# A seam between two network layers: x1 written over the head values, two row tiles held back, and stores and row sums moved to other queues

## The chip, the cores and the metric

The kernel runs on one core of a Trainium2 chip. TensorE multiplies matrices, VectorE and ScalarE do elementwise work, GpSimd and SyncE are used here for little but issuing transfers. The metric is the device time of one execution in microseconds, as the median of several runs.

## What is computed

Eight batches of 2048 rows of 256 features go through two layers, each followed by an addition of its input and a layer norm. All batches share one 2048 x 2048 adjacency mask.

```python
# layer 0: additive attention, 8 heads of 32 features
e    = leaky_relu(e_src[..., :, None] + e_dst[..., None, :], 0.2) + softplus(beta) * log(adj + 1e-6)
attn = softmax(where(adj > 0, e, lowest))
x1   = layernorm(x + concat_heads(attn @ x_proj) @ W_out.T)
# layer 1: dot-product attention
e2   = leaky_relu((x1 @ W1) @ (x1 @ W2).T, 0.2)
out  = layernorm(x1 + relu(softmax(where(adj > 0, e2, -1e12)) @ (x1 @ W3)))
```

## The kernel before

**Layer 0** (class `Gat`, one object per batch). `project` makes the projected values `v` and the factors `re` and `c`; for batches 1 to 7 this is done ahead, during batch 0, and the results are put aside in device memory (`v_d`, `re_d`, `c_d`). The main loop has 64 units per batch: 4 head pairs (`hp`) times 16 tiles of 128 source rows (`jt`). A unit (`step`) loads a 1 MB tile `mt` of the mask's factors, VectorE makes one tile `s` of 128 x 2048 for each of the two heads (L311, from a pool of four buffers), and TensorE multiplies them by the values into `val` (PSUM) and by the weights of the row sums into `den` (L336). For some `jt` the row sums are gathered instead by VectorE and ScalarE in two tiles `d` (L318, L324), which TensorE adds at the end.

After a head pair's 16th unit comes `finish`: ScalarE copies `val` to `ht` and `den` to `dn`; four small transfers put the row sums into `rc` (L353), VectorE takes the reciprocal (L354), one transfer stores it to `rec_d` (L355), and after every second head pair four transfers spread it over the partitions as `rb` (L361), with which VectorE multiplies `ht` (L363). `rb` and `d` share a pool of two buffers.

`output` has 16 row tiles. For each, TensorE multiplies `ht` by the output weights (`y`, L376), VectorE adds x (L378), which was loaded into the tile `h3` (L372), `layer_norm` runs (two VectorE instructions, five on ScalarE, L202 to L210), and x1 goes to device memory (`x1_d`, L380). `turn` then transposes each row tile of x1 into `x1t` (L391, L392) and multiplies by W3 (L396); the result takes the place of x1 in `h3` (L398). `h3` and `x1t` have one buffer each.

**Layer 1** (class `Dot`). For each of 16 row tiles, `scores` makes `e` on TensorE (L426), ScalarE puts it through the leaky relu into `p` (L428), VectorE adds the mask and takes the maximum (L431), and ScalarE takes the exponential (L432). `step` transposes `p` in four groups (`pt`, L445), which ScalarE copies out of PSUM (`pts`, L447), and multiplies by `h3` into `acc` (L461). Between the first group and the product it makes the scores of the next row tile. An epilogue (L464 to L471) divides, applies relu, adds x1, normalises and stores.

**The order.** TensorE executes in the order in which the program writes its instructions. A scheduler orders the other engines and the queues when the kernel is built, by the same priorities and its estimates. `step` of `Dot` takes a function `fill(k)` that is called at three places in it, and with which units of layer 0 of the next batch are put between the parts of layer 1 of this one. The work at a change of batch, from the last head pair's end to the first step of the new `Dot`, is called the seam here. There one row tile of the old `Dot` is held back, to be done first:

```python
if dot is not None:
    dot.step()
layer_0(2)
for k, _ in enumerate(gat.output()):
    if k % 8 == 7:
        layer_0(1)
for k, _ in enumerate(gat.turn()):
    if k % 2 == 1:
        layer_0(1)
```

In the first seam there is no `Dot` yet, and in the last no further batch, so `layer_0` does nothing there. Every transfer is issued by SyncE, from one queue in order.

Of the kernel before, what the change touches and what calls it, by code (L numbers as in the profile page):

```python
# [9 lines left out]
F32 = mybir.dt.float32  # L10
# [8 lines left out]
P = 128  # L19
# [8 lines left out]
def kernel(  # L28
# [26 lines left out]
    nc = tc.nc  # L55
    B, N, D = x.shape
    H, _, DH = w_proj.shape
    NT = N // P
    KC = D // P
    BK = 512  # L60
    NB = N // BK
    HALF = N // 2
    HP = 2
    NP = H // HP
    IG = BK // P
# [5 lines left out]
    whole = ctx.enter_context(tc.tile_pool(name="whole", bufs=1))  # L71
    wide = ctx.enter_context(tc.tile_pool(name="wide", bufs=2))
    chunk = ctx.enter_context(tc.tile_pool(name="chunk", bufs=2))
# [4 lines left out]
    def mm_tile(name):  # L78
        return ps.tile([P, BK], F32, tag="mm", name=name)

    def wide_tile(name, tag, bufs, dtype=F32):
        return wide.tile([P, N], dtype, tag=tag, name=name, bufs=bufs)
# [6 lines left out]
    ident = const.tile([P, P], F32)  # L89
# [39 lines left out]
    wot = const.tile([P, KC, D], F32)  # L129
# [28 lines left out]
    v_d = dram.tile([B, P, NT, D], F32, name="v_d")  # L158
    re_d = dram.tile([B, P, 2, NT, H], F32, name="re_d")
    rec_d = dram.tile([B, NP, 4, HALF], F32, name="rec_d")  # L160
    x1_d = dram.tile([B, N, D], F32, name="x1_d")
# [37 lines left out]
    def layer_norm(z):  # L199

        st = small.tile([P, nc.vector.BN_STATS_DIM], F32, name="st", bufs=2)
        nc.vector.bn_stats(st, z)  # L202
        mv = small.tile([P, nc.vector.BN_AGGR_DIM], F32, name="mv", bufs=3)
        nc.vector.bn_aggr(mv, st)  # L204
        f = small.tile([P, 4], F32, name="f", bufs=3)
        nc.scalar.activation(f[:, 0:1], mv[:, 1:2], AF.Ln, bias=eps_ln)  # L206
        nc.scalar.activation(f[:, 1:2], f[:, 0:1], AF.Exp, scale=-0.5)
        nc.scalar.mul(f[:, 2:3], mv[:, 0:1], -1.0)
        nc.scalar.activation(f[:, 3:4], f[:, 1:2], AF.Identity, scale=f[:, 2:3])
        nc.scalar.activation(z, z, AF.Identity, bias=f[:, 3:4], scale=f[:, 1:2])  # L210

    def row_tile(name, bufs=4):
        return small.tile([P, D], F32, tag="row", name=name, bufs=bufs)


    class Gat:


        def __init__(self, b):
            self.b = b  # L220
            self.units = ((hp, jt) for hp in range(NP) for jt in range(NT))
            self.hts = []
            self.mts = []

        def project(self):
# [56 lines left out]

        def load(self):
            self.v = whole.tile([P, NT, D], F32, name="v")
            nc.sync.dma_start(self.v, v_d[self.b])
            self.re = small.tile([P, 2, NT, H], F32, name="re", bufs=2)
            nc.sync.dma_start(self.re, re_d[self.b])

        def query_rows(self, h):

# [49 lines left out]
        def finish(self, hp):  # L340


            b, lo = self.b, hp % 2 * HP * DH
            if lo == 0:
                self.hts.append(whole.tile([P, N], F32, name=f"ht{hp // 2}"))
            ht = self.hts[-1]
            for s in range(2):
                nc.scalar.copy(ht[lo:lo + HP * DH, ts(s, HALF)], self.val[ts(s, HP * DH), :])
            dn = chunk.tile([P, HALF], F32, tag="ht", name="dn", bufs=3)
            nc.scalar.copy(dn, self.den)  # L350
            rc = small.tile([P, HALF // DH], F32, name="rc", bufs=1)
            for q in range(4):
                nc.sync.dma_start(rc[ts(q, DH), :], dn[q * DH:q * DH + 1, :])  # L353
            nc.vector.reciprocal(rc, rc)  # L354
            nc.sync.dma_start(rec_d[b, hp].rearrange("q (p c) -> (q p) c", c=HALF // DH), rc)  # L355
            if lo == 0:
                return
            rb = wide_tile("rb", "d", 2)
            for a in range(2 * HP):
                src = rec_d[b, hp - 1 + a // HP, a % HP::HP, :]  # L360
                nc.sync.dma_start(rb[ts(a, DH), :].rearrange("p (s i) -> p s i", s=2),  # L361
                                  bass.AP(tensor=src.tensor, offset=src.offset, ap=[[0, DH]] + list(src.ap)))
            nc.vector.tensor_mul(ht, ht, rb)  # L363

        def output(self):


            b = self.b
            self.h3 = h3 = whole.tile([P, NT, D], F32, tag="h3", name="h3")
            xb = x[b].rearrange("(t p) d -> p t d", p=P)  # L370
            for g in range(NB):
                nc.sync.dma_start(h3[:, ts(g, IG), :], xb[:, ts(g, IG), :])  # L372
            for it in range(NT):
                y = mm_tile("y")
                for g, ht in enumerate(self.hts):
                    nc.tensor.matmul(y[:, 0:D], ht[:, ts(it, P)], wot[:, g, :], start=(g == 0), stop=(g == 1))  # L376
                z = h3[:, it, :]
                nc.vector.tensor_add(z, y[:, 0:D], z)  # L378
                layer_norm(z)
                nc.sync.dma_start(x1_d[b, ts(it, P), :], z)  # L380
                yield

        def turn(self):

            self.x1t = x1t = whole.tile([P, KC, N], F32, tag="x1t", name="x1t")
            h3 = self.h3
            for it in range(NT + 1):
                if it < NT:
                    t = mm_tile("tr1")
                    for kc in range(KC):  # L390
                        nc.tensor.transpose(t[:, ts(kc, P)], h3[:, it, ts(kc, P)], ident)  # L391
                    nc.scalar.copy(x1t[:, :, ts(it, P)], t[:, 0:D].rearrange("p (k i) -> p k i", k=KC))  # L392
                if it > 0:
                    t = mm_tile("h3p")
                    for kc in range(KC):
                        nc.tensor.matmul(t[:, 0:D], x1t[:, kc, ts(it - 1, P)], w3s[:, kc, :],  # L396
                                         start=(kc == 0), stop=(kc == KC - 1))
                    nc.scalar.copy(h3[:, it - 1, :], t[:, 0:D])  # L398
                    yield


    class Dot:
# [32 lines left out]
        def step(self, fill=lambda k: None):  # L435


            it, (p, den) = self.at, self.ahead
            self.at += 1
            fill(0)  # L440

            def turned(g):
                t = mm_tile("pt")
                for k in range(IG):
                    nc.tensor.transpose(t[:, ts(k, P)], p[:, ts(g * IG + k, P)], ident)  # L445
                pt = chunk.tile([P, BK], F32, tag="pt", name="pts", bufs=2)
                nc.scalar.copy(pt, t)  # L447
                return pt

            pt = turned(0)  # L450
            if it + 1 < NT:
                if (it + 1) % IG == 0:
                    self.queries((it + 1) // IG)
                self.scores(it + 1)
            fill(1)
            acc = pacc.tile([P, D], F32, tag="acc", name="acc")
            for g in range(NB):
                now, pt = pt, turned(g + 1) if g + 1 < NB else None
                for k in range(IG):
                    j = g * IG + k  # L460
                    nc.tensor.matmul(acc, now[:, ts(k, P)], self.h3[:, j, :], start=(j == 0), stop=(j == NT - 1))  # L461
            fill(2)
            rec = small.tile([P, 1], F32, name="rec1", bufs=2)
            nc.vector.reciprocal(rec, den)  # L464
            xr = row_tile("x1r")
            nc.sync.dma_start(xr, x1_d[self.b, ts(it, P), :])
            z = row_tile("z")
            nc.scalar.activation(z, acc, AF.Relu, scale=rec)  # L468
            nc.vector.tensor_add(z, z, xr)  # L469
            layer_norm(z)  # L470
            nc.sync.dma_start(out[self.b, ts(it, P), :], z)  # L471


    gats = [Gat(b) for b in range(B)]
# [15 lines left out]
    dot = None  # L490
    for b in range(1, B + 1):
        gat, fresh = gats[b - 1], gats[b] if b < B else None

        def layer_0(count):
            if fresh:
                fresh.step(count)

        if fresh:
            fresh.load()
        if dot is not None:  # L500
            dot.step()
        layer_0(2)
        for k, _ in enumerate(gat.output()):
            if k % 8 == 7:
                layer_0(1)
        for k, _ in enumerate(gat.turn()):
            if k % 2 == 1:
                layer_0(1)
        dot = Dot(gat)
        dot.step(lambda k: layer_0((2, 1, 1)[k]))  # L510
        for i in range(NT - 2):
            dot.step(lambda k: layer_0((0, 2 - (i % 2 == 1), 2 - (i % 14 == 13))[k]))
    dot.step()


# [29 lines left out]
```

## Time and profile before

| | |
|---|---|
| time, median of 3 | 4468.5 us (4466.72 to 4468.73) |
| span of the profiled execution | 4465.4 us |
| TensorE, VectorE, ScalarE, GpSimd busy | 96%, 81%, 39%, 0% |
| granted TensorE clock, mean | 0.984 |
| moved by transfers | 843.62 MB, 189 GB/s |

The times in the views are microseconds, durations in groups of instructions nanoseconds. A line of the waits reads: engine and line that waited, the instruction it waited for, the total, how often, and the longest. A line of the timeline reads: start, duration, engine, line, operation, result <- operands, count of merged instructions, and in brackets the idle time before them. `SPq` is SyncE's queue of transfers, and its duration is that of the issue alone. A line `A:B` of the table of stretches gives the length, and then each engine's busy time in it with the number of instructions.

### The profile page before, as it was taken

Reading aid. Unit: us, or ns where it says so; the run is one execution under the profiler, and the core shown is the slowest. Engines: PE = TensorE matmul, PEld = TensorE weight load, DVE = VectorE, ACT = ScalarE, POOL = GpSimd, SP = SyncE. Lnnn points to the kernel's source line nnn. Section 1 sums busy time; section 2 is a strip of 40 time slices with the busy share of each in tenths; the row PEclk is TensorE's granted clock in tenths of the full one; section 3 lists DMA queues with packets and bytes.
Section 4 is the critical chain, followed back from the end, with each engine's and each line's share of the span. In section 5 each row is a group of like instructions: output and inputs, shape, how many; then the busy total and the mean of one; then the engine's idle time right before and its main releaser. Section 6 shows DMA issues by size and latency. Waiting matters only on the chain.

```text
span 4465.4 us, 60558 instructions
## 1 busy us (share of the span) xinstructions
PE 4267.6 (96%) x24988; PEld 2217.3 (50%) x24988; DVE 3631.8 (81%) x2605; ACT 1758.7 (39%) x3611; POOL 7.5 (0%) x14
## 2 busy tenths in 40 slices
PE   6899899999999999999999999999999999999899
PEld 4444344445455545555455544545454554554566
DVE  5778798888989988988899888888988888898222
ACT  5622233334333343334333343333433343333555
POOL 0000000000000000000000000000000000000000
PEclk8999999999999999999999999999999999999999
DMA  7777665666555555556555565555545565553211
GB/s 217 262 264 263 249 218 204 220 233 217 180 189 193 182 193 184 188 181 224 176 182 178 186 213 187 189 181 207 194 160 190 189 216 183 187 182 134 69 50 41
DMA packets 252773, 843.62 MB, mean 189 GB/s; under 512 B 33616, under 2 KB 152400, under 8 KB 176976
## 3 DMA queue, kind: packets, MB, share of 16 engines
q1 hardware_dynamic: 252496, 839.74, 54.0%
q8 instruction: 196, 3.21, 0.3%
q14 instruction: 81, 0.66, 0.0%
HBM read 763.76 MB, written 75.37 MB: 188 GB/s over the span
## 4 chain that ended last, share of the span: by engine, by line
PE 60%; DVE 14%; issue 8%; ACT 4%; DMA 1%; SPq 0%; DVEq 0%; ACTq 0%
PE acc L461 17%; PE e L426 15%; PE val L336 12%; DVE s L311 9%; PE den L336 8%; PE pt L445 4%; DVE d L318 3%; PE h1p L416 2%; ACT p L432 1%; PE h3p L396 1%; ACT h L210 1%; DVE p L431 1%; PE y L376 1%; DMA mt<-mt_d 0%; ACT f L206 0%
## 5 line engine op out<-in xcount | busy, mean ns | idle before, releaser
L311 DVE SCALAR_TENSOR_TENSOR s<-c,re,mt 128x2048 f32<-128x2048 f32 x1024 | 2350.6, 2343 | 209.6 <-PE den L336 159.9
L336 PE MATMUL val<-s,v 128*32 128x512 f32 x8192 | 1045.3, 607 | 78.7 <-DVE s L311 78.5
L461 PE MATMUL acc<-h,pts 128*128 128x256 f32 x4096 | 950.6, 380 | 14.9 <-ACT pts L447 14.4
L426 PE MATMUL e<-x1t,h 128*128 128x512 f32 x2048 | 904.0, 594 | 0.0
L461 PEld LDWEIGHTS acc<-h,pts 128*128 128x128 f32 x4096 | 748.2, 190 | 107.7 <-ACT pts L447 21.8
L336 PE MATMUL den<-s,re 128*32 128x512 f32 x5568 | 709.2, 598 | 0.0
L318 DVE SCALAR_TENSOR_TENSOR d<-s,re,d 128x2048 f32<-128x2048 f32 x272 | 632.4, 2343 | 0.0
L426 PEld LDWEIGHTS e<-x1t,h 128*128 128x128 f32 x2048 | 379.6, 190 | 450.1 <-issue 417.9
L336 PEld LDWEIGHTS val<-s,v 128*32 128x32 f32 x8192 | 240.9, 110 | 697.8 <-issue 526.3
L447 ACT COPY pts<-pt 128x512 f32<-128x512 f32 x512 | 296.1, 583 | 664.7 <-PE pt L445 664.4
L428 ACT ACTIVATE p<-e 128x512 f32<-128x512 f32 x512 | 302.5, 595 | 432.3 <-PE e L426 432.3
L431 DVE CUSTOM_DVE_ANT_0 p<-p,pen 128x2048 f32<-128x2048 f32 x128 | 292.7, 2287 | 205.9 <-ACT p L428 205.6
L336 PEld LDWEIGHTS den<-s,re 128*32 128x32 f32 x5568 | 194.2, 112 | 426.7 <-issue 426.6
L432 ACT ACTIVATE p<-p,neg 128x2048 f32<-128x2048 f32 x128 | 256.7, 2005 | 272.5 <-DVE neg L431 272.5
L445 PEld LDWEIGHTS pt<-ident,p 128*128 128x128 f32 x2048 | 238.0, 141 | 223.5 <-issue 167.2
L445 PE MATMUL pt<-ident,p 128*128 128x128 f32 x2048 | 318.7, 279 | 5.4 <-ACT p L432 5.4
L469 DVE TENSOR_TENSOR z<-z,x1r 128x256 f32<-128x256 f32 x128 | 54.0, 422 | 205.4 <-ACT z L468 197.0
L468 ACT ACTIVATE z<-acc,rec 128x256 f32<-128x256 f32 x128 | 60.6, 473 | 355.9 <-PE acc L461 330.3
L376 PE MATMUL y<-wot,ht 128*128 128x256 f32 x512 | 129.6, 414 | 37.4 <-DVE ht L363 36.3
L206 ACT ACTIVATE f<-mv,eps_ln 128x1 f32<-128x1 f32 x256 | 74.2, 290 | 199.0 <-DVE mv L204 198.1
L396 PE MATMUL h3p<-w3s,x1t 128*128 128x256 f32 x512 | 133.4, 386 | 12.3 <-ACT x1t L392 12.3
L376 PEld LDWEIGHTS y<-wot,ht 128*128 128x128 f32 x512 | 104.7, 208 | 68.3 <-DVE ht L363 39.2
(76 smaller groups left out, 2083.6 us busy)
## 6 DMA issues: line engine op xcount, KB each, us to landing
mt<-mt_d SPq DMA_DIRECT2D x496, 1024.0 KB, 4.8
c<-c_d SPq DMA_DIRECT2D x64, 1024.0 KB, 6.7
pen<-pen_d SPq DMA_DIRECT2D x112, 512.0 KB, 3.3
xr<-in_x_dram SPq DMA_DIRECT2D x16, 1024.0 KB, 7.1
adj_t<-in_adj_dram SPq DMA_DIRECT2D x16, 1024.0 KB, 6.8
mt_d<-mt SPq DMA_DIRECT2D x16, 1024.0 KB, 5.6
rb<-rec_d SPq DMA_DIRECT2D x64, 256.0 KB, 4.0
h<-in_x_dram SPq DMA_DIRECT2D x32, 512.0 KB, 5.9
```

The lines of the kernel that those rows point to most:

```text
L311: nc.vector.scalar_tensor_tensor(sa, self.cs[a], self.re[:, 0, jt, h:h + 1], mt, ALU.max, ALU.mult)
L318: nc.vector.scalar_tensor_tensor(d, sa, e[:, jt - 1, h:h + 1], d, ALU.mult, ALU.add)
L336: nc.tensor.matmul(dst[ts(q, DH), ts(c, BK)], weights[q % 2], s[q % 2][:, ds(q // 2 * HALF + c * BK, BK)], start=start, stop=stop)
L376: nc.tensor.matmul(y[:, 0:D], ht[:, ts(it, P)], wot[:, g, :], start=(g == 0), stop=(g == 1))
L396: nc.tensor.matmul(t[:, 0:D], x1t[:, kc, ts(it - 1, P)], w3s[:, kc, :], start=(kc == 0), stop=(kc == KC - 1))
L426: nc.tensor.matmul(t, self.h1[:, kc, ts(it % IG, P)], self.x1t[:, kc, ts(c, BK)], start=(kc == 0), stop=(kc == KC - 1))
L428: nc.scalar.activation(p[:, ts(c, BK)], t, AF.Prelu, alpha=ALPHA)
L431: nc.vector.tensor_tensor_reduce(p, p, pen, -1.0, FMAX, ALU.add, ALU.min, neg)
L432: nc.scalar.activation(p, p, AF.Exp, bias=neg, scale=-1.0, accum_out=den)
L445: nc.tensor.transpose(t[:, ts(k, P)], p[:, ts(g * IG + k, P)], ident)
L447: nc.scalar.copy(pt, t)
L461: nc.tensor.matmul(acc, now[:, ts(k, P)], self.h3[:, j, :], start=(j == 0), stop=(j == NT - 1))
```

## The change

Four things are done together.

1. x1 is written over the head values. `ht` of both head groups becomes one tile, laid out so that the 256 columns that row tile `it` read of it are contiguous (`self.ht[:, it]`), and `output` writes x1 into them. x comes through tiles `xg` from the pool `ht` of small tiles (three buffers). `h3` is not needed until `turn`, so `output` doesn't wait for the old `Dot` to be done with it.
2. Two row tiles of layer 1 are held back for the seam. The first (with the last scores in it) is done with two layer-0 units at its end; into the second the 16 row tiles of `output` are put as 5, 5 and 6, with two units. The remaining units are spread over 13 steps rather than 14.
3. ScalarE issues the stores of x1 and of the output, and the four transfers `rc` of row sums.
4. GpSimd issues `rec_d`, `rb`, and the loads of `v` and `re`.

It is meant to give the normalisation of the head values time to finish behind other work, to cover the row tiles of `output` with products of layer 1, and to keep transfers that wait for a result out of the queue that loads operands.

```diff
 def load(self):
-            nc.sync.dma_start(self.v, v_d[self.b])
+            nc.gpsimd.dma_start(self.v, v_d[self.b])
-            nc.sync.dma_start(self.re, re_d[self.b])
+            nc.gpsimd.dma_start(self.re, re_d[self.b])
 def finish(self, hp):
-            if lo == 0:
-                self.hts.append(whole.tile([P, N], F32, name=f"ht{hp // 2}"))
-            ht = self.hts[-1]
+            if hp == 0:
+                self.ht = whole.tile([P, NT, KC, P], F32, tag="heads", name="ht")
+            ht = self.ht[:, :, hp // 2, :]
...
-                nc.sync.dma_start(rc[ts(q, DH), :], dn[q * DH:q * DH + 1, :])
+                nc.scalar.dma_start(rc[ts(q, DH), :], dn[q * DH:q * DH + 1, :])
...
-            nc.sync.dma_start(rec_d[b, hp].rearrange("q (p c) -> (q p) c", c=HALF // DH), rc)
+            nc.gpsimd.dma_start(rec_d[b, hp].rearrange("q (p c) -> (q p) c", c=HALF // DH), rc)
...
-                nc.sync.dma_start(rb[ts(a, DH), :].rearrange("p (s i) -> p s i", s=2),
+                nc.gpsimd.dma_start(rb[ts(a, DH), :].rearrange("p (s i) -> p s i", s=2),
...
 def output(self):
+            def load(g):
+                xs.append(chunk.tile([P, IG, D], F32, tag="ht", name="xg", bufs=3))
+                nc.sync.dma_start(xs[g], xb[:, ts(g, IG), :])
+            for g in range(NB - 1):
+                load(g)
             for it in range(NT):
+                if it == IG:
+                    load(NB - 1)
                 y = mm_tile("y")
...
-                z = h3[:, it, :]
-                nc.vector.tensor_add(z, y[:, 0:D], z)
+                z = self.ht[:, it].rearrange("p g i -> p (g i)")
+                nc.vector.tensor_add(z, y[:, 0:D], xs[it // IG][:, it % IG, :])
                 layer_norm(z)
-                nc.sync.dma_start(x1_d[b, ts(it, P), :], z)
+                nc.scalar.dma_start(x1_d[b, ts(it, P), :], z)
...
 def step(self, fill=lambda k: None):
...
-            nc.sync.dma_start(out[self.b, ts(it, P), :], z)
+            nc.scalar.dma_start(out[self.b, ts(it, P), :], z)
...
-        if dot is not None:
-            dot.step()
-        layer_0(2)
-        for k, _ in enumerate(gat.output()):
-            if k % 8 == 7:
-                layer_0(1)
+        if dot is None:
+            layer_0(2)
+            for k in range(NT):
+                output(1)
+                if k % 8 == 7:
+                    layer_0(1)
+        else:
+            dot.step(lambda k: layer_0((0, 0, 2)[k]))
+            dot.step(lambda k: (output((5, 5, 6)[k]), layer_0((0, 1, 1)[k])))
...
-        for i in range(NT - 2):
-            dot.step(lambda k: layer_0((0, 2 - (i % 2 == 1), 2 - (i % 14 == 13))[k]))
+        for i in range(NT - 3):
+            dot.step(lambda k: layer_0((0, 2 - (i % 3 == 2), 2)[k]))
     dot.step()
+    dot.step()
```

## What I expected

> **What bounds the kernel now.** I read the page's engine shares first, then the busy time of stretches laid around the batch changes, then TensorE's waits inside those stretches, and last the timeline of two of them.
>
> ```profile
> PE 4267.6 (96%) x24988; PEld 2217.3 (50%) x24988; DVE 3631.8 (81%) x2605; ACT 1758.7 (39%) x3611; POOL 7.5 (0%) x14
> ```
>
> TensorE leaves 4465.4 - 4267.6 = 198 us idle. The change adds and removes no matmul, so only this idle time is for sale. Where is it?
>
> ```profile
> 0.00:360.00 360.00, 285.93 (x1930) 151.11 (x1934) 258.31 (x144) 164.13 (x327) 6.38 (x11) 0.93 0.75 251
> ...
> 1060.00:1160.00 100.00, 90.42 (x524) 47.83 (x525) 88.64 (x86) 40.57 (x128) 0.00 (x0) 0.98 0.58 193
> 1160.00:1570.00 410.00, 408.62 (x2420) 206.65 (x2419) 362.54 (x234) 157.21 (x268) 0.00 (x0) 1.00 0.53 189
> ...
> 4130.00:4215.00 85.00, 65.45 (x264) 47.22 (x261) 20.68 (x57) 42.63 (x138) 0.00 (x0) 0.90 0.24 73
> ```
>
> The columns after the length are PE, PEld, DVE, ACT and POOL busy, then clock, DMA share and GB/s. Between two seams TensorE lacks only 1.4 us in 410. The first 360 us (batch 0's layer 0 alone) lack 74 us, and the change hardly touches their order. What is left is mostly the seams: 9.6 us in this one and much the same in the five like it, 19.6 in the last (batch 7, nothing to cover it). The first four lines below are TensorE's waits of 1060 to 1160 us (all six middle seams read alike), the next those of 4130 to 4215 us:
>
> ```profile
> PE y L376 <- DVE ht L363: 4.6, 1, 4.6
> PE val L336 <- DVE s L311: 3.7, 5, 1.2
> PE h3p L396 <- ACT x1t L392: 1.0, 2, 0.8
> PE acc L461 <- ACT pts L447: 0.6, 1, 0.6
> ```
> ```profile
> PE y L376 <- DVE ht L363: 8.9, 1, 8.9
> PE pt L445 <- ACT p L432: 5.1, 1, 5.1
> PE h3p L396 <- ACT x1t L392: 4.9, 1, 4.9
> PE acc L461 <- ACT pts L447: 0.6, 1, 0.6
> ```
>
> So 6 x 9.9 + 19.5 = 79 us are within reach of the re-ordering: 36.5 of them the wait for the normalised head values, 22.2 (6 x 3.7) that for VectorE's s tiles in the turn. The chain behind the first, in the last seam's timeline:
>
> ```profile
> 4128.38 1.90 PE L336 MATMUL den<-d,ones 128*32 128x512 f32 x16
> ...
> 4131.41 2.40 SPq L353 DMA_DIRECT2D rc<-dn  x4
> ...
> 4135.49 0.34 SPq L355 DMA_DIRECT2D rec_d<-rc  x1
> ...
> 4140.49 0.93 SPq L361 DMA_DIRECT2D rb<-rec_d  x2
> ...
> 4146.94 2.29 DVE L363 TENSOR_TENSOR ht<-ht,rb 128x2048 f32<-128x2048 f32 x1 [5.32 <-DMA rb<-rec_d]
> ```
>
> The row sums leave TensorE at 4130.2, ht is ready at 4149.2: 19 us, of which the held step covers 10. The last two rb transfers are issued at 4140.5 because SyncE stood at a load of x into h3 (L372), whose buffer the last step's matmuls were reading. In the middle seams the chain is the same 20 us (1058.6 to 1078.8), there with a 4.6 us pair of L311 ahead of the multiplication on VectorE.
>
> **What the Trainium skill says.** DMA: Bandwidth & Descriptors, Issuing engines are not separate DMA queues: another issuer saves issue time on the sequencer only. The trace agrees so far that SyncE's order, not bandwidth, held rb back (DMA share 0.24 there). The same page, SWDGE vs HWDGE vs iDMA: transfers issued by GpSimd get descriptors from software, those of ScalarE from hardware as SyncE's do; Latency and other measured facts gives a first byte after about 1 us against 0.6. No GpSimd transfer is in this trace. SBUF — State Buffer, Who interferes with whom: descriptor generation is held up by two-port VectorE modes, not by two-input instructions (its own inference). The L311 instructions that fill VectorE have two tile inputs and take 2343 ns for 2048 columns, so I expect no blocking; unmeasured here. TensorE: Matmul & The Clock Gate, Architectural detail: ScalarE and VectorE are strict FIFO. The timeline agrees: ScalarE sat 7.3 us at a copy of s into d (L324) that waited for ht.
>
> **The change part by part.**
>
> *Two held row tiles (14 and 15).* From the end of the sums (call it 0) TensorE did pt and acc of one step (about 10 us) and, in the middle, two layer-0 units (2 x 3.5). Now step 14 still has its scores: 10 + 7.1 (L426: 904.0/128) = 17, then two units, so the first y comes at 24 us, against 20 for the chain. In the last seam there are no units: 17 against 19. If the chain is unchanged, the wait is 0 and 2 us: 36.5 saved less 2.
>
> *Route of the chain.* rc by ScalarE: right behind dn; SyncE also issued within 0.3 us of it, so equal. rec_d and rb by GpSimd: five starts, each 0.4 us dearer by the page's 1 - 0.6 (estimate), two of them in series or up to five: +0.8 to +2. Against that SyncE's block falls away (rb could have gone at 4138 rather than 4140.5: -2.5). I take zero net and 0.5 us residue per middle seam: 3. Other bound: GpSimd takes 4 us more, 4 us residue per seam.
>
> *Room for VectorE.* From 0 to the turn VectorE now has p of step 15 (2.4), four units (4 x 4.7), the multiplication 2.3, 16 rows (L378, L202, L204: 0.41 + 0.42 + 0.18 = 1.0 each) and two short epilogues: 43 us, beside TensorE's 17 + 7 + 16 + 10 + 7 = 57. Before, the rows stood in a stretch where VectorE was full. So it enters the turn a unit or more ahead; four s buffers hold two units, 9 us, and the turn's deficit was 3.7. I leave 0.7 per seam: saved 6 x 3.0 = 18.
>
> *Rows inside step 15: ScalarE.* This is the new wait. In the last seam ScalarE streamed one layer_norm per 1.05 us (starts of L210, 4157.7 to 4165.2 for seven rows). The store behind it now costs ScalarE its issue, 0.32 us by SyncE's row below, and most often a wait for its own z: 1.42 a row.
>
> ```profile
> L353 SPq DMA_DIRECT2D rc<-dn x128: 507/588/610, 214.3 to 4133.2; - x128
> L380 SPq DMA_DIRECT2D x_d<-h x128: 319/320/407, 564.2 to 4170.9; - x128
> L471 SPq DMA_DIRECT2D out_dram<-z x128: 337/338/425, 673.9 to 4462.7; - x128
> ```
>
> Queued behind rows 0 to 9 are the pts copies of step 15, and acc waits for the second. TensorE asks for it after 10 rows (9.8), two pt (0.9), one unit (3.6), one acc group (1.8) and a pt (0.45): 16.6 us. ScalarE starts 2.4 us late (1078.83 to 1081.23), ten rows 14.2, two copies 1.1: 17.7; with an L311 pair of VectorE in between (4.7), up to 22. I take 2 us in place of 0.6. Likewise x1t behind rows 10 to 15 and the step's own epilogue: ScalarE 2.4 + 8.5 = 10.9 to 12.8, TensorE 5.9 + 3.6 + 0.5 = 10.0: 1.8 in place of 1.0. In the last seam, with no units: pts asked for at 13.0, there at 17.7, wait 4.7; x1t 5, as before; p (5.1) stays.
>
> *Stores and rc on ScalarE elsewhere.* 128 x 0.338 + 128 x 0.32 + 128 x 0.588 = 160 us more on an engine with 39% load. Out stores lie beside scores, where TensorE has three PSUM tiles (4.1 us) of lead. The four rc issues (2.35 us) come between dn and the next pt copy: 1.2 + 2.35 + 0.6 = 4.2 against 4.1 when scores follow; I charge 0.2 for two of four head pairs in seven batches, 3 us in all.
>
> *x1 in place, other transfers.* No store has to land before h3 is written (waits of 0.5 us once), and SyncE no longer stands at z (698 us of queue waits at L471), but VectorE waited for mt only 19.9 us from 600 to 4130 us and is not the bound: nothing. In the first seam (540 to 600 us) TensorE waited 9.9 us for s behind c loads issued after the four rc (2.4 us): 2 saved. Unit counts per batch stay 64; 48 in 13 steps rather than 14 make 3.7 a step: VectorE 3.7 x 5.8 + 3.4 = 24.9 us, TensorE 3.7 x 3.5 + 17.9 = 30.9, still hidden.
>
> *Sum.* Middle seams: 9.9 - (0.5 + 0.7 + 2 + 1.8) = 4.9, times 6 = 29.4. Last: 19.5 - (2 + 4.7 + 5 + 5.1) = 2.7. First: 2. Less 3: 31. 4468.5 - 31 = 4437.
>
> **The rivals.**
> 1. ScalarE keeps up (pts copies get ahead of the rows): waits of 0.5 + 0.7 + 0.6 per middle seam and 10 in the last: 6 x 8.1 + 9.5 + 2 = 60, 4408. For: an engine at 39%. Against: in the last seam it was full for 10 us on end and made h3p wait 4.9.
> 2. GpSimd's transfers are late: 4 us per middle seam stay, so that 9.9 becomes 4 + 0.7 + 2 + 1.8 = 8.5, and nothing is saved in the last: 6 x 1.4 = 8, 4460. For: no such transfer has been seen here; against: the chain has 4 us of room.
> 3. ScalarE's issues stand on the path in every step: with a third of the 160 us, 53 - 31 = 22 lost, 4490; with half, 4517. For: FIFO order; against: TensorE waited for pts 1 to 2 us per 410 us stretch.
>
> **How the numbers follow.** Forecast 0.50, rival 1 0.22, rival 2 0.16, rival 3 0.12. The range runs from a little below rival 1 to just beyond rival 2: 4402 to 4466; beyond it lie rival 3 and, at 0.08, a recovery still larger. Faster (below 4459.6): forecast, rival 1, half of rival 2: 0.80. Same: the other half, 0.08. Slower: 0.12.
>
> **What would show it.** The waits of a middle seam: y for ht below 1 us, val for s about 1, acc for pts about 2, sum about 5; in the last seam ht about 2 and pts about 5. Stretches between seams still lack 1 to 3 us in 410. I am wrong if those lack more than 5 (rival 3), if ht still ends a wait of 4 us (rival 2), or if VectorE still ends 3 us of the turn.

## The result, and the profile after

The kernel after takes 4532.0 us (4528.98 to 4532.63) against 4467.6 for the kernel before on the same chip: 1.0143 times as long, 95% interval 1.0126 to 1.0161. It is slower by 64 us where 31 us less were forecast. First the page of the kernel after: busy times, then the queues (packets, MB, share of 16 engines).

```profile
PE 4268.1 (94%) x24988; PEld 2229.3 (49%) x24988; DVE 3626.2 (80%) x2605; ACT 1756.2 (39%) x3611; POOL 68.3 (2%) x124
...
q1 hardware_dynamic: 197744, 772.73, 48.8%
q0 software_dynamic: 7488, 32.91, 2.5%
q10 hardware_dynamic: 43008, 34.10, 2.3%
```

TensorE is busy for the same 4268 us; what grew is its idle time, from 198 to 259 us. Transfers now run in three queues: q1 is SyncE's, q0 GpSimd's, q10 ScalarE's. The table of stretches says where the idle time is:

```profile
1060.00:1160.00 100.00, 82.22 (x484) 47.95 (x477) 69.38 (x83) 44.12 (x129) 4.38 (x7) 0.91 0.62 205
1170.00:1570.00 400.00, 396.43 (x2328) 196.19 (x2327) 363.61 (x227) 147.99 (x252) 3.90 (x7) 1.00 0.53 184
```

Between the seams it is quiet (3.6 us in 400); a middle seam lacks 17.8 us in 100, where it lacked 9.6. In windows of 150 us laid around each seam the six middle ones lack 15.5 to 19.8 us against some 10 before, which makes 42 of the 61 us; the first seam adds 7, batch 0 ahead of it 6, the stretches between the seams 6, the last seam nothing. TensorE's waits in two middle seams of the kernel after (1010 to 1160 us and 1570 to 1690 us), and in the last (4160 to 4270 us):

```profile
PE y L383 <- DVE ht L363: 9.4, 1, 9.4
PE h3p L403 <- ACT x1t L399: 4.9, 1, 4.9
PE y L383 <- DVE ht L385: 2.6, 2, 1.9
```
```profile
PE h3p L403 <- ACT x1t L399: 5.1, 1, 5.1
PE y L383 <- DVE ht L363: 3.4, 1, 3.4
PE acc L468 <- ACT pts L454: 2.8, 2, 1.9
PE y L383 <- DVE ht L385: 2.4, 2, 1.7
```
```profile
PE h3p L403 <- ACT x1t L399: 6.9, 1, 6.9
PE pt L452 <- ACT p L439: 5.2, 1, 5.2
PE acc L468 <- ACT pts L454: 3.9, 2, 3.6
PE y L383 <- DVE ht L363: 3.8, 1, 3.8
```

The wait for the normalised head values, which the held step was to cover, is still there: 9.4, 3.4, 4.2, 2.7, 4.8 and 2.0 us in the six middle seams, 26.5 together, where it was 4.6 in each before. Two waits are new or grew: h3p for ScalarE's copy x1t (1.0 before), and y for the row tile's addition (L385), which frees the PSUM tile. The wait of acc for pts grew less. The timeline of the chain in the seam of 1570 us, kernel after:

```profile
1585.72 5.18 ACTq L353 DMA_DIRECT2D rc<-dn  x4
1597.44 0.35 DVE L354 RECIPROCAL rc<-rc 128x32 f32<-128x32 f32 x1 [8.81 <-DMA rc<-dn]
1598.08 0.57 POOL L355 DMA_DIRECT2D rec_d<-rc  x1 [12.63 <-DVE rc L354]
...
1604.25 1.06 POOL L361 DMA_DIRECT2D rb<-rec_d  x2 [5.04 <-DMA rec_d<-rc]
1611.58 2.29 DVE L363 TENSOR_TENSOR ht<-ht,rb 128x2048 f32<-128x2048 f32 x1 [5.34 <-DMA rb<-rec_d]
```

From the first rc to ht it is 28 us. No instruction in it is long: each of the three transfers lands late, 8.8, 5.0 and 5.3 us after VectorE or GpSimd was free for it. The issue of rc takes longer too, 5.2 us for four where SyncE took 2.4: in five of the six middle seams ScalarE issued the fourth 2.9 to 3.7 us after the third, and here the trace names the landing of an out store as what it stood for. The transfers' medians from issue to landing (last column), before and then after:

```profile
rb<-rec_d SPq DMA_DIRECT2D x64, 256.0 KB, 4.0
...
rc<-dn SPq DMA_DIRECT2D x128, 4.0 KB, 2.5
rec_d<-rc SPq DMA_DIRECT2D x32, 16.0 KB, 2.3
```
```profile
rb<-rec_d POOLq DMA_DIRECT2D x64, 256.0 KB, 6.6
...
rc<-dn ACTq DMA_DIRECT2D x128, 4.0 KB, 5.3
...
rec_d<-rc POOLq DMA_DIRECT2D x32, 16.0 KB, 4.0
```

### The profile page after: what moved, and what is told of

Same layout as the page of the kernel before. It is cut to its first block, busy times and chain, and to the rows that moved or that the text cites. A ratio compares the mean times of both kernels' runs of the same rounds, so it can differ in the third digit from the quotient of the medians.

```text
span 4527.1 us, 60718 instructions
## 1 busy us (share of the span) xinstructions
PE 4268.1 (94%) x24988; PEld 2229.3 (49%) x24988; DVE 3626.2 (80%) x2605; ACT 1756.2 (39%) x3611; POOL 68.3 (2%) x124
## 4 chain that ended last, share of the span: by engine, by line
PE 54%; DVE 15%; issue 9%; DMA 7%; ACT 4%; ACTq 1%; POOL 0%; DVEq 0%; POOLq 0%
PE acc L468 15%; PE e L433 13%; PE val L335 11%; DVE s L310 9%; PE den L335 7%; PE pt L452 4%; DVE d L317 4%; PE h1p L423 2%; DMA rc<-dn 2%; DMA mt<-mt_d 1%; DMA rb<-rec_d 1%; PE h3p L403 1%; DMA out_dram<-z 1%; DMA rec_d<-rc 1%; ACT f L206 1%
## 5 line engine op out<-in xcount | busy, mean ns | idle before, releaser
L335 PE MATMUL val<-s,v 128*32 128x512 f32 x8192 | 1017.8, 606 | 63.7 <-DVE s L310 56.6
L335 PE MATMUL den<-s,re 128*32 128x512 f32 x5568 | 689.3, 595 | 3.1 <-ACT dn L350 3.1
L403 PE MATMUL h3p<-w3s,x1t 128*128 128x256 f32 x512 | 145.0, 412 | 42.0 <-ACT x1t L399 42.0
```

The lines of the kernel that those rows point to most:

```text
L335: nc.tensor.matmul(dst[ts(q, DH), ts(c, BK)], weights[q % 2], s[q % 2][:, ds(q // 2 * HALF + c * BK, BK)], start=start, stop=stop)
```

## The experiments

Fifteen variants, each timed beside the kernel before (4467.4 to 4468.9 us). Idle and busy are TensorE's in the profiled execution; before it was 198 idle and 4268 busy.

| | who issues what | us | ratio to before (95%) | idle | busy |
|---|---|---|---|---|---|
| after | ScalarE: rc, x1, out; GpSimd: rec_d, rb, v, re | 4532.0 | 1.0143 (1.0126 to 1.0161) | 259 | 4268 |
| e1 | SyncE: all | 4477.8 | 1.0021 (1.0013 to 1.0030) | 206 | 4266 |
| e2 | ScalarE: rc, x1, out | 4482.1 | 1.0033 (1.0020 to 1.0046) | 216 | 4266 |
| e3 | GpSimd: rec_d, rb, v, re | 4483.1 | 1.0041 (1.0028 to 1.0054) | 225 | 4256 |
| e4 | old order, queues as after | 4528.6 | 1.0138 (1.0123 to 1.0153) | 261 | 4267 |
| e5 | as after, v and re by SyncE | 4533.1 | 1.0143 (1.0128 to 1.0158) | 262 | 4269 |
| e6 | as after, rec_d and rb by SyncE | 4496.9 | 1.0065 (1.0050 to 1.0080) | 233 | 4262 |
| e7 | as after, stores by SyncE | 4478.3 | 1.0024 (1.0013 to 1.0035) | 221 | 4262 |
| e8 | as after, stores, v and re by SyncE | 4477.4 | 1.0019 (1.0011 to 1.0027) | 221 | 4259 |
| e9 | ScalarE: rc; GpSimd: x1, out | 4452.5 | 0.9969 (0.9960 to 0.9978) | 195 | 4262 |
| e10 | GpSimd: x1, out | 4437.5 | 0.9931 (0.9916 to 0.9946) | 180 | 4246 |
| e11 | old order, GpSimd: x1, out | 4466.9 | 1.0000 (0.9991 to 1.0008) | 199 | 4265 |
| e12 | GpSimd: out | 4432.8 | 0.9924 (0.9910 to 0.9939) | 178 | 4249 |
| e13 | ScalarE: x1; GpSimd: out | 4467.3 | 0.9995 (0.9986 to 1.0003) | 204 | 4264 |
| e14 | ScalarE: out | 4444.8 | 0.9947 (0.9933 to 0.9962) | 184 | 4255 |
| e15 | GpSimd: rec_d, rb, out | 4469.2 | 1.0002 (0.9993 to 1.0011) | 214 | 4260 |

What a row doesn't name is issued by SyncE, and where no order is named it is the new one.

**Order or queues? (e1 to e4)** Against the kernel after, e1 gives all seven transfers back to SyncE, e2 GpSimd's four, e3 ScalarE's three; e4 is the kernel before with the queues of the kernel after.

```diff
 # e1: all of these; e2: those of gpsimd; e3: those of scalar
-            nc.gpsimd.dma_start(self.v, v_d[self.b])
+            nc.sync.dma_start(self.v, v_d[self.b])
...
-                nc.scalar.dma_start(x1_d[b, ts(it, P), :], z)
+                nc.sync.dma_start(x1_d[b, ts(it, P), :], z)
 # e4, in the kernel before
-                nc.sync.dma_start(rc[ts(q, DH), :], dn[q * DH:q * DH + 1, :])
+                nc.scalar.dma_start(rc[ts(q, DH), :], dn[q * DH:q * DH + 1, :])
...
```

> The changed kernel with every transfer back on SyncE's queue: only x1 in place and the two held row tiles are left of the change. Theory G (GpSimd's queue: the load of v in a queue of its own is served packet by packet in turn with the small rc and x transfers and stretches the row-sum chain to 31 us) and theory S (the stores and rc on ScalarE make x1t and pts wait) both put the loss on the queues: 4425 to 4445 us, waits of y for ht below 10 us in all. Theory R (the new order itself loses: 16 rows, pts and x1t meet on ScalarE and VectorE whoever issues the stores): 4500 us or more, waits of h3p for x1t still over 30 us.

> The changed kernel with rec_d, rb, v and re back on SyncE; ScalarE keeps the stores and rc. Theory G: the waits of y for ht (40.5 us) and of val for v (6.8) go, 4480 to 4490 us, rc lands in about 3 us. Theory S: little changes, 4515 us or more, and h3p still waits 40 us for x1t. Theory R: as S.

> The changed kernel with the stores and rc back on SyncE; GpSimd keeps rec_d, rb, v and re. Theory S: the wait of h3p for x1t falls from 42 to about 15 us, those of y for L385 (15.4) and acc for pts (20) to 10 together, 4480 to 4490 us. Theory G: ht stays at 30 us or more, 4505 us or more. Theory R: 4525 us.

> The kernel before with the queue moves alone (stores and rc by ScalarE; rec_d, rb, v, re by GpSimd), its order and buffers as they were. Theory G: the chain grows by about 11 us at a place with less to cover it, each middle seam loses 8 to 11 us, 4530 to 4550 us. Theory S: about 1 us in each row of output and little else, 4475 to 4490 us. Theory R: within 5 us of the kernel before, 4463 to 4473 us.

The queues alone cost 60 us in the old order, and with them the new order is no faster than the old (4532 and 4529). But the new order with one queue (e1) didn't gain either. Its time lies in none of the ranges expected. Its middle seams lack 7.8 to 8.6 us rather than some 10, with no wait for ht; one wait per batch has come between the seams, val for s, 4.3 us. Its timeline, run e1:

```profile
1334.46 0.36 SPq L478 DMA_DIRECT2D out_dram<-z  x1
...
1335.34 0.92 SPq L183 DMA_DIRECT2D mt<-mt_d  x2
...
1341.55 2.35 DVE L310 SCALAR_TENSOR_TENSOR s<-c,re,mt 128x2048 f32<-128x2048 f32 x1 [6.35 <-DMA mt<-mt_d]
```

SyncE had issued nothing since the rb transfers of that head pair (their last issue ended at 1327.8). It stood at the out store until ScalarE had finished z (1334.4); the mt loads queued behind it, and VectorE waited 6.35 us for mt. The stretches between the seams lack some 5 us in e1. In e2 and e3, which each take something off SyncE, they lack 1.0 to 3.5 (after batch 0), and yet both end where e1 does, each with a cost of its own. In e3 rc came 11 to 14 us after its issue in the middle seams, although SyncE had issued it; VectorE stood at the reciprocal, and the mask, the exponential and pts of the step came late behind it (acc waited up to 7.4 us for pts).

**Which of GpSimd's transfers? (e5, e6)** The load of v is 2 MB and lies in the same queue as the sums.

```diff
 # e5
-            nc.gpsimd.dma_start(self.v, v_d[self.b])
+            nc.sync.dma_start(self.v, v_d[self.b])
 # e6
-            nc.gpsimd.dma_start(rec_d[b, hp].rearrange("q (p c) -> (q p) c", c=HALF // DH), rc)
+            nc.sync.dma_start(rec_d[b, hp].rearrange("q (p c) -> (q p) c", c=HALF // DH), rc)
 # (and re in e5, rb in e6, likewise)
```

> The changed kernel with the loads of v and re alone back on SyncE. Theory V (the load of v in a queue of its own, taken packet by packet in turn with rc, holds the row sums back): y waits for ht less than 8 us in all (40.5 with the change), rc lands in under 4 us at the seams, 4482 to 4492 us. Theory P (rec_d and rb are late because GpSimd issues them): ht still 25 us or more, 4510 us or more.

> The changed kernel with rec_d and rb alone back on SyncE; v and re stay on GpSimd, rc and the stores on ScalarE. Theory V: rc still lands 8 us or more after its issue at the seams, ht keeps 20 us or more, 4505 us or more. Theory P: ht below 8 us, 4482 to 4492 us.

Moving v changes nothing: 4533.1, with rb landing in 7.6 us, so theory V is out. Moving the sums takes 35 us off, as theory P had it (the time is 5 us above its range), and takes the wait for ht out of the middle seams from the second on; what stays is ScalarE's part. Waits of run e6, 1560 to 1690 us:

```profile
PE h3p L403 <- ACT x1t L399: 5.0, 1, 5.0
PE y L383 <- DVE ht L385: 2.8, 2, 1.8
```

**The stores (e7, e8)**

```diff
 # e7; e8 also v and re
-                nc.scalar.dma_start(x1_d[b, ts(it, P), :], z)
+                nc.sync.dma_start(x1_d[b, ts(it, P), :], z)
-            nc.scalar.dma_start(out[self.b, ts(it, P), :], z)
+            nc.sync.dma_start(out[self.b, ts(it, P), :], z)
```

> The changed kernel with the stores of x1 and of the output back on SyncE; rc stays on ScalarE, GpSimd's transfers as in the change. Theory S1 (a store costs ScalarE 0.4 us a row, and x1t waits behind six rows): the wait of h3p for x1t falls from 42 to about 18 us, 4500 to 4512 us with the ht waits left as they are. Theory S2 (x1t waits because the rows come late after ht, whoever stores): x1t stays over 30 us, 4525 us or more.

> The changed kernel with v, re and the stores on SyncE: only the row sums leave its queue (rc by ScalarE, rec_d and rb by GpSimd). If V and S1 hold, both new waits are gone (ht below 8 us, x1t below 20 us), and so is the wait of 4.3 us for s that each batch has once where all is on SyncE: 4440 to 4455 us, faster than the kernel before. If P holds, ht keeps 25 us: 4475 us or more.

54 us less with the stores alone back, 22 below the range of theory S1, which had the right waits. In a middle seam of e7 h3p waits 2.3 us for x1t rather than 5.1, and y 0.2 rather than 2.4 for the addition, while ht and pts each still end a wait of 3.4. e8 ends where e7 does (4477.4), with 4 to 5 us of waiting for ht in most middle seams: again the place of v is worth nothing, and the sums stay late. SyncE's standing at out stores does no harm in e7, where the stretches between seams lack 1.0 us in 360, nor in the kernel before. In e1 an out store stood behind the sums' transfers and ahead of the loads of mt; that this order makes the difference was not tried by itself.

**The good places (e9 to e12)** GpSimd has next to nothing else to do, so a store that waits there should block nobody. e9 leaves rc on ScalarE, e10 puts it on SyncE, e12 leaves only the out stores off SyncE; e11 is e10's stores in the old order.

```diff
 # e10, against e1; e9 has rc by nc.scalar; e12 has only the second
-                nc.sync.dma_start(x1_d[b, ts(it, P), :], z)
+                nc.gpsimd.dma_start(x1_d[b, ts(it, P), :], z)
-            nc.sync.dma_start(out[self.b, ts(it, P), :], z)
+            nc.gpsimd.dma_start(out[self.b, ts(it, P), :], z)
 # e11: the same two, in the kernel before
```

> The kernel after, with rec_d, rb, v and re on SyncE, rc left on ScalarE, and both stores (x1, out) moved from ScalarE to the idle GpSimd. Theory A (the chain of row sums is slow only because rec_d and rb go by a queue of their own, and the stores cost only ScalarE's time in order; SyncE is held up only by the out stores): y waits 0 to 1 us for ht in the middle seams, h3p waits about 2 us for x1t rather than 5, the stretches between seams lack about 1 us, time 4448 to 4460. Theory B (any second queue with bulk in it slows the chain, whoever feeds it): rb lands in 6 us or more and y waits 3 us or more for ht, time 4475 to 4500.

> The kernel after, with every transfer on SyncE except the stores of x1 and out, which GpSimd issues. Theory A (what the all-SyncE version of the new order still loses is SyncE standing at an out store with loads of mt behind it, 4.3 us per batch, 7 batches): those waits of val for s go, no wait for ht, time 4478 - 30 = 4448, 4443 to 4455. Theory C (the wait has another cause, VectorE being short of time there): the stretches between seams still lack about 5 us in 360, time 4470 to 4480.

> The kernel before, its order unchanged, with the stores of x1 and out issued by GpSimd. Theory A (before loses about 1 us between seams, so SyncE's standing at stores costs it nothing there; only in the seams could it help): 4460 to 4470, and the difference to the run with the same queues in the new order, 10 to 20 us, is what the re-ordering is worth. Theory D (the stores' place is the whole gain, the order gives nothing): the time is that of the new order with these queues, within 5 us.

> The kernel after, with every transfer on SyncE except the out stores, which GpSimd issues (the stores of x1 on SyncE). Theory A (the out stores alone hold up SyncE between the seams): the 4.3 us wait per batch goes, time within 5 us of the run with both stores on GpSimd. Theory E (the x1 stores, which wait for their layer norm in the seam, hold up the loads of mt and x behind them too): 8 us or more above that run, with waits of val for s or y for x in the seams.

e12 beats both kernels, at 4432.8. The old order gains nothing from the same stores (e11 against before), so with the queues of e10 the re-ordering is worth 29 us (e11 - e10), more than the 10 to 20 expected. e1 and e12 differ in one line and by 45 us: the out stores alone held SyncE up. e9 and e12 came out much as theory A had it; e10 fell 5 us below its range. A middle seam of run e12 (waits of 1540 to 1670 us, then the chain in the timeline):

```profile
PE val L335 <- DVE s L310: 3.1, 3, 1.2
PE h3p L403 <- ACT x1t L399: 2.0, 1, 2.0
PE y L383 <- ACT pts L454: 1.6, 1, 1.6
PE y L383 <- DVE ht L385: 1.0, 1, 1.0
```
```profile
1554.99 2.41 SPq L353 DMA_DIRECT2D rc<-dn  x4
...
1558.99 0.35 DVE L354 RECIPROCAL rc<-rc 128x32 f32<-128x32 f32 x1 [1.09 <-DMA rc<-dn]
1559.37 0.33 SPq L355 DMA_DIRECT2D rec_d<-rc  x1
...
1562.25 3.08 SPq L374 DMA_DIRECT2D xg<-in_x_dram  x3
...
1567.51 2.29 DVE L363 TENSOR_TENSOR ht<-ht,rb 128x2048 f32<-128x2048 f32 x1 [0.73 <-DMA rb<-rec_d]
...
1574.75 4.58 PE L383 MATMUL y<-wot,ht 128*128 128x256 f32 x20
```

The same four steps take 15 us rather than 28, and ht is ready 5 us before TensorE gets to y.

**Why the sums land late.** In one queue in order, nothing is issued behind the chain until the chain is through: above, x (`xg`) comes after the rb's, and the issue before rc was that of v, 4.5 us earlier. In the kernel after, SyncE is free to go on loading while the chain runs in other queues. Its timeline in the seam of 1570 us, then the stretches from issue to landing of rec_d there (1598.08) and between the seams (1750.90), and the same in the kernel before, in a seam (1574.84) and between (1710.34); the last three numbers of a line are clock, DMA share and GB/s:

```profile
1584.13 4.84 SPq L183 DMA_DIRECT2D mt<-mt_d  x2
1597.41 0.93 SPq L374 DMA_DIRECT2D xg<-in_x_dram  x2
```
```profile
1598.08:1603.96 5.88, 3.98 (x21) 3.19 (x20) 2.02 (x3) 2.56 (x3) 1.12 (x2) 1.00 0.96 279
1750.90:1752.60 1.70, 1.70 (x24) 0.50 (x18) 0.80 (x1) 0.86 (x2) 0.56 (x1) 1.00 0.04 10
```
```profile
1574.84:1576.42 1.58, 1.58 (x11) 1.40 (x10) 0.00 (x0) 1.58 (x2) 0.00 (x0) 1.00 0.26 65
1710.34:1714.23 3.89, 3.89 (x22) 1.28 (x24) 0.94 (x1) 2.24 (x4) 0.00 (x0) 1.00 0.66 255
```

Issued by GpSimd, rec_d lands in 1.7 us when the DMA engines are nearly empty and in 5.9 when they are full; issued by SyncE it takes 1.6 us with few loads beside it and 3.9 with many. So the load on the DMA engines explains far more than the issuer does. The rb's, back on SyncE in e6 but with loads of x issued among them, take 6.2 us in the median there, about as long as by GpSimd. The seam is a quiet place in the kernel before, because its one queue stands at the chain, and a crowded one in the kernel after. The late rec_d spends 3.9 us before its first packet starts (1.1 in the quick one). VectorE, which the prediction thought of as a possible hindrance to GpSimd's descriptors, was busy for 34% of the late transfer and 47% of the quick one, so it is not what makes the difference here. A run in which SyncE's loads are held back while the chain runs on GpSimd was not made; the cause is read from the traces.

**Each move by itself, against e12 (e13 to e15)**

```diff
 # e13
-                nc.sync.dma_start(x1_d[b, ts(it, P), :], z)
+                nc.scalar.dma_start(x1_d[b, ts(it, P), :], z)
 # e14
-            nc.gpsimd.dma_start(out[self.b, ts(it, P), :], z)
+            nc.scalar.dma_start(out[self.b, ts(it, P), :], z)
 # e15 (and rb likewise)
-            nc.sync.dma_start(rec_d[b, hp].rearrange("q (p c) -> (q p) c", c=HALF // DH), rc)
+            nc.gpsimd.dma_start(rec_d[b, hp].rearrange("q (p c) -> (q p) c", c=HALF // DH), rc)
```

> The run with only the out stores on GpSimd (4432.8), with one change: the stores of x1 go to ScalarE. Theory S1 (the dear stores are those of x1, which stand between the layer norms of the seam and so delay x1t and the addition's buffers): h3p waits 4 to 5 us for x1t in the middle seams, y waits 1 to 3 us for the addition, 3 to 5 us per seam and time 4452 to 4465. Theory S2 (they cost their issue alone, 0.33 us beside other work, and the out stores are dear): 4430 to 4440.

> The run with only the out stores on GpSimd (4432.8), with one change: the out stores go to ScalarE, the stores of x1 stay on SyncE. Theory S1 (the stores of x1 are the dear ones): one out store per step is hidden, 4430 to 4440. Theory S2 (an out store in ScalarE's order delays the pts copies of every step): acc waits for pts grow by 1 to 2 us per seam and stretch, time 4450 to 4465.

> The run with only the out stores on GpSimd (4432.8), with one change: rec_d and rb are issued by GpSimd, rc staying on SyncE. Theory Q (a small transfer on a queue of its own lands late beside bulk on another queue, and the chain of the sums has no room for it): rec_d lands in about 4 us and rb in 6 to 7, y waits 3 to 5 us for ht in the middle seams, and because the pause is over 4 us the granted clock falls to 0.6 to 0.8 for some 8 us behind it, so 4465 to 4490. Theory P' (only rc being late too used up the room): y waits at most 1 us for ht, 4430 to 4445.

The waits of 1560 to 1690 us, run e13 and then run e15:

```profile
PE h3p L403 <- ACT x1t L399: 4.6, 1, 4.6
...
PE y L383 <- DVE ht L385: 3.0, 2, 1.9
```
```profile
PE y L383 <- DVE ht L363: 4.8, 1, 4.8
PE h3p L403 <- ACT x1t L399: 2.3, 1, 2.3
```

e13 shows the waits that were expected of dear x1 stores, with a time just above its range. e15 came out much as theory Q had it: it keeps rc on SyncE, and still ht is late, so GpSimd's transfers need no help from rc. e14 falls between the two expectations. The waits of theory S2 are not there: in its middle seams the wait of y moved from pts (1.6 us) to the addition (2.9 to 3.8 in most), with 8.0 to 8.9 us idle in most, where e12 has 7.6 to 8.5. Of its 6 us more idle time 4 lie between the seams (1.5 to 1.6 us in most stretches against 1.0), 2 in the middle seams and 2 in the first, with 2 less elsewhere; another 6 us are busy time, with 5 clock dips against 3 (see below).

The single costs are then: x1 by ScalarE 34.5 (e13 - e12), rec_d and rb by GpSimd 36.4 (e15 - e12), rc by ScalarE 15.0 (e9 - e10), out by ScalarE rather than GpSimd 12.1 (e14 - e12), v and re by GpSimd -1.1 (after - e5): 97, and after - e12 is 99. That they add up so well is partly luck, since with the out stores on SyncE they don't (e1 to e3, e7), and since the kernel before moves by 1.5 us between these groups of runs. Taken back one at a time from the kernel after, the stores weigh more (54, e7) than rec_d and rb (35, e6). The 15 us of rc are the least certain: the two profiled executions lie 31 us apart. In them e9 has 13 us more idle time up to the end of the first seam and less in the middle seams (6.5 to 7.7 us against 7.8 to 8.4), and 16 us more busy time with 10 clock dips against 2.

**Idle time is half of it.** e12 gains 20 us of TensorE's idle time and 18 us of its busy time with the same matmuls. Most of the second part is in the clock column of the table of stretches. The kernel before in its seam of 1570 us and once more in its turn, then e12, in stretches of 3.4 us:

```profile
1583.53:1586.95 3.42, 1.38 (x10) 0.30 (x2) 3.42 (x2) 0.00 (x0) 0.00 (x0) 1.00 0.75 249
...
1590.36:1593.77 3.41, 3.41 (x9) 2.69 (x9) 2.07 (x6) 2.71 (x7) 0.00 (x0) 0.50 0.79 317
1593.77:1597.19 3.42, 3.42 (x17) 3.01 (x17) 3.11 (x11) 2.90 (x13) 0.00 (x0) 1.00 0.23 77
...
1651.80:1655.21 3.41, 1.36 (x7) 0.29 (x10) 3.41 (x3) 0.37 (x1) 0.00 (x0) 1.00 0.00 0
1655.21:1658.63 3.42, 3.42 (x20) 0.85 (x16) 3.42 (x2) 0.00 (x0) 0.00 (x0) 0.50 0.72 266
```
```profile
1582.24:1585.65 3.41, 1.81 (x9) 1.44 (x8) 3.41 (x10) 3.32 (x13) 0.00 (x0) 1.00 1.07 376
1585.65:1589.06 3.41, 2.38 (x16) 0.56 (x18) 3.41 (x6) 2.39 (x12) 0.00 (x0) 1.00 0.83 293
```

After before's pause of 4.6 us (1584.9 to 1589.5) the clock is 0.50 from 1587 to 1593.8, and TensorE, busy throughout the stretch, does 9 matmuls of y there and 17 in the next. The second dip came with two pauses of 0.8 and 1.2 us. The clock records of the seventeen profiled executions hold only 0.5 and 1.0, and nearly all low stretches last 3.4 us or a small multiple of it. Laid on that grid from 560 to 4030 us, each of the 162 dips that begin there came after a stretch of 3.4 us in which TensorE had been idle for 1.73 us or more, and in none of the 16826 stretches after which the clock stayed at 1.00 was it idle for more than 1.94. So in these runs 1.95 us of idle time within one such stretch always brought a dip and less than 1.7 never did, in one piece or two; e12's pauses of 1.6 and 1.0 us, in two stretches, stay below it.

In stretches of 2 us from 560 to 4030 us there are 11 such dips in the kernel before, 15 after, 9 in e13, 11 in e15, 2 in e10 and 3 in e12. The Trainium skill has this: TensorE: Matmul & The Clock Gate, Part 1: The HAM clock gate, says that the array's clock is halved after an idle window of some 3.4 us. The traces agree in the half and in the 3.4 us, but a window that was idle for little more than half was enough here. Over the whole span the dips cost 50 us of TensorE's busy time in the kernel before and 38 in e12 (half of the busy time at 0.50, worked out from the clock records), so 12 of the 18 us are the clock's. The other 6 are not explained, and busy time does not follow the dips alone: the kernel after loses 69 us in them and is busy for as long as the kernel before.

## Why the prediction was wrong

**"Route of the chain" failed, and was the largest error.** It set rc as "equal" and rec_d and rb as "zero net" with 0.5 us of residue, by pricing GpSimd's start alone. The single moves put 36 us on rec_d and rb and 15 on rc: y waited 2.0 to 9.4 us for ht in a middle seam, 4.4 in the mean, to a bound of 4. What it left out is how long the transfers take to land. The 20 us of the chain were measured with SyncE's queue standing at it, so with rec_d landing in 1.6 us; off that queue the chain runs beside SyncE's loads, and rec_d takes 5.9. The prediction looked at the load on the DMA engines in the last seam (share 0.24), where no load for a next batch runs, and not in a middle seam.

The sentence of the Trainium skill that the prediction leaned on (DMA: Bandwidth & Descriptors, Issuing engines are not separate DMA queues) says what another issuer can save; that it can lose was not asked. The same page, Queues, rings and completion order, says that each DMA engine takes turns between queues packet by packet. That fits the packet records where three queues are busy: from 1586 to 1588 us they show 43 packets of GpSimd's queue with 16 KB each (v), 45 of SyncE's and 43 of ScalarE's (a store; rc lies behind it in the same queue). How much of the late landing is this turn-taking was not tried by itself. In the last seam rec_d still takes 3.6 us by GpSimd against 1.9 by SyncE, but there too the engines are fuller, with a DMA share of 0.78 against 0.33 while it is under way.

**"Rows inside step 15: ScalarE" had the mechanism right and the size wrong.** ScalarE's rate was as forecast, 7 layer norms, six of them with a store, from 1124.7 to 1134.5 us, 1.40 each. But the last unit before h3p has no row sums of its own and took TensorE 1.9 us, not 3.6, and x1t was waited for 4.8 to 5.1 us in the middle seams, not 1.8. The wait of y for the addition, 1.9 to 3.5 us a seam, was not foreseen at all. pts was right (2 forecast, 0.9 to 2.8 measured). The x1 stores alone cost 34.5 us.

**"Stores and rc on ScalarE elsewhere" was mis-sized.** Between the seams 6 us were lost in all where 3 were charged, so the stretches there stayed nearly as quiet as forecast (3.6 in 400). But rc costs 15 us, which e9 shows as idle time up to the first seam and as clock dips, not as longer waits in the middle seams; why the dips come stays open. The out stores cost 12, spread over all stretches, and which of ScalarE's instructions they delay stays open too.

**"Room for VectorE" was half right.** In place of 3.7 us a seam, s ended waits of at most 2.1 in the kernel after and of 3.1 in e12 (6.0 in its first middle seam), where 0.7 was forecast; in e12 it is the largest wait that is left.

**"Two held row tiles" was right.** With all of the sums' transfers on SyncE ht ends no wait in the middle seams (e1, e12). In the last seam 3.8 us stood against the 2 forecast (3.6 in e1 and e12, too); that seam as a whole took 19.8 where 16.8 were forecast.

**"x1 in place, other transfers" was right for the old order only.** SyncE's wait at z was counted as harmless, and in the old order it is (e11). In the new order with one queue it costs 45 us (e1 - e12). So taking the out stores off SyncE is needed for the re-ordering to pay, which the prediction did not see; in the kernel after that wait was gone, and the rest outweighed it.

**A term was missing: the clock.** Every pause was priced at its own length. The good version of the change gains 35 us, close to the forecast of 31, but that is luck: half of it is busy time, most of that from dips that no longer occur. Of the rivals, GpSimd's lateness (the second) named the right place and, with 4 us a middle seam, nearly the wait that came (4.4); its time of 4460 was far off because it kept the forecast's 1.8 us for x1t and had nothing for the addition, the first seam and the clock. The third came nearest in time (4490 to 4517) by a mechanism that the quiet stretches rule out.

## What to carry to other kernels

Take the load on the DMA engines from the very stretch in which a dependent chain of small transfers will run, and ask what the change itself will put beside it. A chain in the bulk loads' own queue holds those loads back while it runs, and may be faster there than in a queue of its own, where each landing can take twice as long or more. Ask of every transfer which waits for a result what stands behind it on the issuing engine: here an idle engine was the place for stores, and one that feeds TensorE was not. And price TensorE's pauses above their own length once they add up to some 2 us within 3.4 us, since the same idle time spread thinner cost less.

## What the runs showed of the hardware that was not expected

- A 16 KB transfer landed in 1.7 us by GpSimd and 1.6 by SyncE where the DMA share was 0.04 and 0.26, and in 5.9 and 3.9 us where it was 0.96 and 0.66. A queue that stood at its own chain kept the share low.
- The clock record holds 0.5 and 1.0 alone. Idle time of 1.95 us or more within one stretch of 3.4 us of that record's grid, in one piece or two, always brought 0.50 in the next, and less than 1.7 never did; a pause of 4.6 us brought 6.8 us of it. 11 such dips against 3 went with 12 of the 18 us of TensorE's busy time between the kernel before and e12.
- A store issued by ScalarE took 0.33 us of issue, and the 128 of x1 (42 us) came to 34.5 us of time on an engine with 39% load, as they stand where its copies are waited for.
